# Weight sums, extra products and a second rotation input in the Householder phase of a fused rotation and transformer kernel

## The chip, the core and the metric

The kernel runs on one core of one Trainium2 chip. The metric is the device time of one execution in microseconds (us). Three runs of the kernel before took 2220.52, 2226.43 and 2232.18 us; their median, 2226.43 us, is the time before. Everything is computed in 32-bit floating point.

## The reference

A batch of 8 sequences of 512 tokens with 576 features is first rotated in a subspace and then goes through one transformer block whose shifts, scales and gates come from a conditioning vector. Cut to what matters:

```python
U, _ = jnp.linalg.qr(P)                       # P: 576 x 64
A    = skew-symmetric 64 x 64 from silu(cond) @ W.T + b     # one per sequence
R    = expm(A)
z    = einsum('btn,nd->btd', x, U)
x    = x + einsum('btd,nd->btn', einsum('btd,bde->bte', z, R) - z, U)
ada  = silu(c) @ ada_w + ada_b                # 6 x 576: shifts, scales, gates
x    = x + gate_msa * attention(modulate(layernorm(x)))     # over the 16 heads of one token
x    = x + gate_mlp * (gelu(modulate(layernorm(x)) @ fc1_w + fc1_b) @ fc2_w + fc2_b)
```

The attention is not over tokens: each token has a 16 x 16 matrix of scores between its own heads, which the kernel makes on VectorE. The MLP's inner width is 2304.

## The kernel before

**The prologue.** The factor U comes from a Householder QR of P, written out in 64 steps (`qr_step`, L217 to L285). Each step has two small TensorE products, `rp` (L220, a row spread over all partitions) and `dp` (L228, column sums by a matrix of ones), a chain of small VectorE instructions (L237 to L283, then the next step's products and sums in `column_products`, L209 and L214), and two ScalarE instructions (L244, L245). A step needs the one before it, so the prologue's length is the sum of the steps.

Between two steps a generator, `beside` (L450), is asked for one piece of other work, which lands in TensorE's queue after the step's `dp` and before the next step's `rp`: the 9 column groups of `ada` (`ada_columns`, L306; five products of 384 columns each), the 8 groups of skew entries (`skew_entries`, L337), the rows of the skew matrices by way of DRAM (`skew_rows`, L349), the modulation columns (`modulation`, L317), and the matrix exponential (`expm`, L370): polynomial terms made on GpSimd, and 19 squarings, each of two products of 64 x 64 blocks (`products`, L362) whose results are copied by ScalarE (L444) and get a constant added by GpSimd (L446). The generator's work ends five steps before the QR does. The order of TensorE, VectorE and ScalarE in the prologue is the order in which the code is written; GpSimd and the DMA queue (SP) are ordered by the framework's planner[...].

After the 64 steps a triangular inverse is made in six levels (L513 to L539), then U and its transpose (L549, L556).

**The block.** Work goes unit by unit: (sequence 0, tile 0), (0, 1), (0, tiles 2 and 3), and then two units of two tiles of 128 tokens for each of the other seven sequences. A unit has the projection of its attention output (`Projection`, L756), a norm, and the MLP; beside it run the qkv products of the next unit (`qkv`, L685), the rotation of the next sequence (`rotation`, L622: `project_z` reads x transposed, `rotate` reads x), and, on VectorE, the attention of the next unit (`attention`, L708). The attention output goes to DRAM (L750) and is read back in another layout (L771); both transfers are issued by SP's queue.

The MLP exists in two forms. `mlp_plain` (L870) makes fc2 with 8 products of 288 columns for each of 9 pairs of blocks and two tiles. `mlp` (L907) is a Strassen-like scheme: 4 products of 288 and 4 of 144 columns per pair, and one of 288 at the end, with sums of activation blocks made on GpSimd (L923 to L926) and sums of fc2's weight blocks read from a DRAM buffer, `comb_d` (L933). Sequence 0 uses `mlp_plain`, the other sequences `mlp`. In the unit of sequence 0 that has two tiles, `mlp_plain` also makes the weight sums, four GpSimd instructions for each pair (`combine_weights`, L859), and stores them to `comb_d` (L868).

From the first unit on, the planner orders every engine. One buffer holds the rotation's transposed input `xT` (L635), five hold normed tokens, and one DMA queue (SP's) carries every transfer.

Of the kernel before, what the change touches and what calls it, by code (L numbers as in the profile page):

```python
# [48 lines left out]
def rotate_then_dit_block(  # L49
# [64 lines left out]
    with tc.manual_schedule(engines=engines), tc.tile_pool(name="prep", bufs=1) as prep, tc.tile_pool(name="qrs", bufs=2) as qrs, tc.tile_pool(  # L114
# [4 lines left out]
        name="ps_ex", bufs=2, space=PSUM  # L119
    ) as ps_ex, tc.tile_pool(name="ps_m", bufs=2, space=PSUM) as ps_m:  # L120
        m = prep.tile([128, NK, R], F32, tag="m", name="m")
# [166 lines left out]
        def paced(n, parts):  # L288

            k = 0  # L290
            for part in parts:
                for _ in part:
                    k += 1
                    if k % n == 0:
                        yield
# [10 lines left out]
        def ada_columns(g):  # L306
# [6 lines left out]
            for k in range(2):  # L313
                if g == (4, 8)[k]:
                    nc.sync.dma_start(out=gates_d[k], in_=ada_rows[:, (3 * k + 2) * D : (3 * k + 3) * D])

        def modulation(v):  # L317
            ps = ps_m.tile([128, NK, B], F32, tag="m", name=f"mod_{v}")
            for c, rows in enumerate(KROWS):
                first = v * D + c * 128  # L320
                nc.tensor.matmul(
                    ps[0:rows, c], lhsT=ada_rows[:, first : first + rows], rhs=ident[0:B, 0:B], start=True, stop=True
                )
            for c0, c1, rows in ((0, 4, 128), (4, 5, 64)):
                dst = mod[0:rows, v // 3 * 2 + v % 3, c0:c1, :]
                if v % 3:
                    nc.scalar.activation(dst, ps[0:rows, c0:c1], AF.Identity, bias=ones[0:rows, 0:1])
                else:
                    nc.scalar.copy(dst, ps[0:rows, c0:c1])
# [120 lines left out]
        def beside():  # L450
            yield
            yield
            yield from paced(4, [ada_columns(g) for g in range(6)])
            yield from paced(4, [skew_entries(g) for g in range(8)])
            skew_rows()
            for v in (0, 1, 3):
                modulation(v)
                yield
            yield
            yield from expm()  # L460
            yield from paced(2, [ada_columns(g) for g in range(6, 9)])
            modulation(4)
            yield

        for g in range(4):
# [9 lines left out]
        for j in range(R):  # L475
            t, done = qr_step(j, t, done)
            if j > 1:
                next(side, None)
            if j == 8:
                load_rows(wqkv, qkv_w, 65)  # L480
                nc.sync.dma_start(out=b2, in_=fc2_b.to_broadcast([128, D]))
                for g in (6, 7, 8):
                    load_ada(g)
        for _ in side:
            pass

# [3 lines left out]
        if True:  # L490
# [24 lines left out]
            nc.vector.scalar_tensor_tensor(ls[1], vv, rd, lower[1], ALU.mult, ALU.mult)  # L515
            nc.vector.tensor_tensor(y_, ident[0:R, 0:R], ls[1], ALU.subtract)
            xps = ps_m.tile([R, R], F32, tag="m", name="xps")
            nc.tensor.matmul(xps, lhsT=y_, rhs=ident[0:R, 0:R], start=True, stop=True)
# [9 lines left out]
            for s in LEVELS[1:]:  # L528
                p1 = ps_qr.tile([R, R], F32, tag="dp", name=f"p1_{s}")
                nc.tensor.matmul(p1, lhsT=ls[s], rhs=x_, start=True, stop=True)  # L530
                p1s = qrs.tile([R, R], F32, tag="p1s", name=f"p1s_{s}")
                nc.vector.tensor_copy(p1s, p1)
                p2t = ps_m.tile([R, R], F32, tag="m", name=f"p2t_{s}")
                nc.tensor.matmul(p2t, lhsT=p1s, rhs=y_, start=True, stop=True)
                if s < LEVELS[-1]:
                    p2 = ps_m.tile([R, R], F32, tag="m", name=f"p2_{s}")
                    nc.tensor.matmul(p2, lhsT=y_, rhs=p1s, start=True, stop=True)
                    nc.vector.tensor_tensor(x_, x_, p2, ALU.subtract)
                nc.vector.tensor_tensor(y_, y_, p2t, ALU.subtract)  # L539


            ps = ps_m.tile([R, R], F32, tag="m", name="s_ps")
            nc.tensor.matmul(ps, lhsT=y_, rhs=vt[:, 0:R], start=True, stop=True)
            sneg = prep.tile([R, 2, R], F32, tag="sneg", name="sneg")
            for h in range(2):
# [39 lines left out]

    xns = padded("xn", 5)
    ats = padded("at", 2)
# [34 lines left out]
    def rotation(b):  # L622


        def project_z(half):
            if half == 0:
                zTs[b] = big.tile([128, S], F32, tag="zT", name=f"zT_{b}")
                p = slice(b // 4 * R, b // 4 * R + R)
                for n in range(2):
# [4 lines left out]
                    nc.scalar.copy(g[0:R, n * HALF : (n + 1) * HALF], gps)  # L634
            xT = xin.tile([128, NK, 256], F32, tag="xT", name=f"xT_{b}_{half}")  # L635
            cols = slice(half * 256, half * 256 + 256)
# [71 lines left out]
    def attention(b, ts):  # L708
# [5 lines left out]
        own = [toks.pop((b, i)) for i in ts]  # L714
        sc2 = small.tile([128, 2, H, H], F32, tag="sc", name=f"sc_{hb}", bufs=2)[:, 0:NU]
        for t, tok in enumerate(own):
# [141 lines left out]

    def combine_weights(g, w2):  # L859

        (b11, b12), (b21, b22) = [(w[:, 0:HALF], w[:, HALF:D]) for w in w2]
        tt = wst.tile([128, 3, HALF], F32, tag="w2t", name=f"tt_{g}", bufs=3)
        t1, t2, t4 = (tt[:, k] for k in range(3))
        nc.gpsimd.tensor_tensor(t1, b12, b11, ALU.subtract)
        nc.gpsimd.tensor_tensor(t2, b22, t1, ALU.subtract)
        nc.gpsimd.tensor_tensor(t3[:, g], b22, b12, ALU.subtract)
        nc.gpsimd.tensor_tensor(t4, t2, b21, ALU.subtract)
        nc.sync.dma_start(out=comb_d[g], in_=tt)  # L868

    def mlp_plain(pr, gate, aside):  # L870
        hb, NU = pr.hb, len(pr.ts)
        acc, gts = {}, {}
        for g in range(NP + 1):
# [8 lines left out]
            for k in range(2):  # L882
# [6 lines left out]
                for t in range(NU):  # L889
                    for n in range(2):  # L890
# [8 lines left out]
                        )  # L899
            if NU == 2:  # L900
                combine_weights(g, w2)
        for t in range(NU):
# [4 lines left out]
    def mlp(pr, gate, aside):  # L907
# [8 lines left out]
        for g in range(NP + 1):  # L916
# [18 lines left out]
            stop = g == NP - 1  # L935
            whole = [(gt[:, 0, 0], wq[:, 0]), (gt[:, 1, 0], wq[:, 1]), (ss[:, 2], wq[:, 2]), (gt[:, 1, 1], wt[:, 2])]
            for k in (0, 1, 3):
                nc.tensor.matmul(p[k], lhsT=whole[k][0], rhs=whole[k][1], start=g == 0, stop=stop)  # L938

            nc.tensor.matmul(p[2], lhsT=whole[2][0], rhs=whole[2][1], start=g == 0, stop=stop)  # L940
            for i, (lhs, rhs) in ((5, (ss[:, 0], wt[:, 0])), (6, (ss[:, 1], wt[:, 1]))):
                for n, bank in enumerate(halves_of[i]):
# [50 lines left out]
    first = rotation(0)  # L993
    now(first[:3])
    feature_major(0, 0)
    now(qkv(0, 0))
    now(first[3:])
    now(qkv(0, 1))
# [4 lines left out]
    for k, (b, ts) in enumerate(units):  # L1003
# [10 lines left out]
        else:  # L1014
            nb, nts = units[k + 1]
            q = qkv(nb, nts[0]) + qkv(nb, nts[1])
        if len(ts) == 1:
            pr.turn(0)
            now(q[:1])
            pr.product(0, 0)  # L1020
            pr.product(0, 1)
            pr.norm(0, gb2)
            now(q[1:3])
            pr.turn_normed((0, 1))
            now(q[3:])
        else:
# [16 lines left out]
        if (k == 1 or k > 2 and ts[0] == 0) and b + 1 < B:  # L1043
# [3 lines left out]
            aside |= {7: lambda: feature_major(b + 1, 0), 8: lambda: feature_major(b + 1, 1)}  # L1047
        (mlp if b else mlp_plain)(pr, gate_m, aside)
        if k + 1 < len(units):
# [54 lines left out]
```

## Time and profile before

| | |
|---|---|
| median of three runs | 2226.43 us (2220.52 to 2232.18) |
| the profiled execution, its own time | 2228.81 us |
| its span, first to last instruction | 2227.0 us |
| mean granted TensorE clock over the span | 0.952 |
| TensorE (PE) busy | 2104.2 us, 94% |
| VectorE (DVE) busy | 1789.4 us, 80% |
| GpSimd (POOL) busy | 679.6 us, 31% |
| ScalarE (ACT) busy | 386.7 us, 17% |
| DMA | 347.58 MB, mean 156 GB/s |

The span falls into three parts: the prologue up to about 247 us, the start of the block up to about 647 us, and a long even part up to the end. A busy share over the whole span says little about the first two. PE is TensorE's products and PEld its loading of the stationary operand; "PEclk" is the clock that the chip granted to TensorE. A product in 32-bit floating point shows as two instruction records. Where a group of records carries a count such as x8, the time is that of the whole group. In the chain of waits each line is the start, the length and what the chain ran through.

### The profile page before, as it was taken

How to read it: one execution, taken by the hardware profiler on the slowest of the kernel's cores; microseconds unless marked ns; L12 is line 12 of the kernel's file. 1: busy time of each engine (PE TensorE's matmuls, PEld its weight loads, DVE VectorE, ACT ScalarE, POOL GpSimd, SP SyncE). 2: the span in 40 equal slices, each digit the busy share in tenths (PEclk: the TensorE clock that was granted, in tenths of full speed). 3: DMA queues.
4: the chain of work that ended last, by engine and by line, in shares of the span. 5: the costliest groups of instructions: out<-in, count | busy, mean ns of one | idle time of the engine just before them, and what ended most of it. 6: DMA issues, size and time to landing. Idle time of an engine off the chain costs nothing.

```text
span 2227.0 us, 26157 instructions
## 1 busy us (share of the span) xinstructions
PE 2104.2 (94%) x9571; PEld 1570.8 (71%) x9571; DVE 1789.4 (80%) x2443; ACT 386.7 (17%) x817; POOL 679.6 (31%) x846
## 2 busy tenths in 40 slices
PE   7788879899799999999999999999999999999998
PEld 3485437666568686868687777777786868686877
DVE  8997399899678797969796979697988889697930
ACT  2232111122021111111111112121211122111110
POOL 2151000113434242424242433324332334242422
PEclk9755789999999999999999999999999999999999
DMA  9101116743647373845565465637373737364654
GB/s 304 30 2 62 50 54 206 249 124 111 186 156 233 107 214 108 251 128 170 155 201 165 153 178 168 205 116 208 128 231 98 215 114 225 111 202 122 200 178 125
DMA packets 211698, 347.58 MB, mean 156 GB/s; under 512 B 82382, under 2 KB 100123, under 8 KB 211572
## 3 DMA queue, kind: packets, MB, share of 16 engines
q1 hardware_dynamic: 211572, 345.92, 51.3%
q8 instruction: 77, 1.26, 0.2%
q14 instruction: 49, 0.40, 0.1%
HBM read 313.46 MB, written 32.39 MB: 155 GB/s over the span
## 4 chain that ended last, share of the span: by engine, by line
PE 65%; DVE 14%; issue 11%; DMA 6%; POOL 3%; ACT 1%; SPq 0%; POOLq 0%; DVEq 0%; ACTq 0%
PE fc L838 26%; PE fc L938 8%; PE qkvp L696 7%; PE fc L943 5%; DVE sc L727 3%; PE fc L940 3%; PE p L953 3%; DMA w<-in_fc_w 3%; PE fc L893 2%; PE ada L310 2%; DMA out<-x 1%; DVE qk L721 1%; PE zps L640 1%; DVE pv L743 1%; DVE att L749 1%
## 5 line engine op out<-in xcount | busy, mean ns | idle before, releaser
L838 PE MATMUL fc<-h2T,w 128*128 128x256 f32 (+3 forms) x3060 | 656.4, 368 | 2.0 <-ACT h2T L814 1.9
L838 PEld LDWEIGHTS fc<-h2T,w 128*128 128x128 f32 (+1 forms) x3060 | 549.4, 191 | 76.8 <-ACT h2T L814 7.0
L696 PE MATMUL qkvp<-wqkv,hT 128*128 128x432 f32 (+1 forms) x1280 | 480.9, 529 | 1.3 <-DVE pt L795 0.9
L721 DVE TENSOR_TENSOR qk<-qkv 128x2304 f32<-128x2304 f32 x128 | 327.3, 2557 | 122.9 <-ACT qkv L703 120.4
L696 PEld LDWEIGHTS qkvp<-wqkv,hT 128*128 128x128 f32 (+1 forms) x1280 | 240.6, 191 | 204.5 <-issue 196.4
L743 DVE TENSOR_TENSOR pv<-sc,qkv 128x2304 f32<-128x2304 f32 x128 | 330.9, 2585 | 3.3
L749 DVE TENSOR_REDUCE att<-pv 128x144 f32<-128x2304 f32 x128 | 326.5, 2551 | 3.3
L727 DVE TENSOR_REDUCE sc<-qk 128x64 f32<-128x2304 f32 x128 | 326.3, 2549 | 2.8
L923 POOL TENSOR_TENSOR ss<-gt 128x128 f32<-128x128 f32 x126 | 135.1, 1072 | 539.4 <-ACT gt L846 539.4
L846 ACT ACTIVATE gt<-fc 128x512 f32<-128x512 f32 (+1 forms) x153 | 87.5, 572 | 725.2 <-PE fc L838 725.0
L703 ACT COPY qkv<-qkvp 128x432 f32<-128x432 f32 x128 | 66.3, 518 | 559.0 <-PE qkvp L696 552.6
L943 PEld LDWEIGHTS fc<-wt,ss 128*128 128x128 f32 x1008 | 140.5, 190 | 13.2
L943 PE MATMUL fc<-wt,ss 128*128 128x144 f32 x1008 | 144.1, 286 | 0.0
L938 PE MATMUL fc<-wq,gt 128*128 128x288 f32 x504 | 142.8, 405 | 0.0
L610 POOL TENSOR_TENSOR rstd_m<-rstd_m,mhalf 128x1 f32<-128x1 f32 x32 | 17.6, 551 | 362.0 <-DVE rstd_m L609 338.3
L969 DVE TENSOR_TENSOR u<-u,fc 128x288 f32<-128x288 f32 x14 | 6.4, 454 | 135.3 <-ACT u L968 135.3
L793 PE MATMUL pj<-w2q_p,aT 128*128 128x288 f32 x384 | 108.5, 419 | 4.0 <-DMA w2q_p<-in_proj_w 2.3
L938 PEld LDWEIGHTS fc<-wq,gt 128*128 128x128 f32 x504 | 94.1, 189 | 19.9
L854 POOL TENSOR_TENSOR x<-x,mt 128x288 f32<-128x288 f32 x64 | 50.8, 796 | 169.5 <-DVE mt L853 169.5
L893 PE MATMUL fc<-w,gt 128*128 128x288 f32 x288 | 82.6, 431 | 20.4 <-DMA w<-in_fc_w 19.8
L925 POOL TENSOR_TENSOR ss<-gt,ss 128x128 f32<-128x128 f32 x126 | 97.7, 776 | 9.9
L793 PEld LDWEIGHTS pj<-w2q_p,aT 128*128 128x128 f32 x384 | 71.7, 194 | 31.5 <-issue 6.2
(223 smaller groups left out, 2381.1 us busy)
## 6 DMA issues: line engine op xcount, KB each, us to landing
w<-in_fc_w SPq DMA_DIRECT2D x306, 320.0 KB, 3.4
wq<-in_fc_q SPq DMA_DIRECT2D x126, 432.0 KB, 3.7
wt<-comb_d SPq DMA_DIRECT2D x126, 432.0 KB, 4.2
w<-in_fc_w SPq DMA_DIRECT2D x54, 288.0 KB, 4.1
w2q_p<-in_proj_w SPq DMA_DIRECT2D x34, 432.0 KB, 3.7
xT<-in_x_t SPq DMA_DIRECT2D x16, 640.0 KB, 10.1
w2t_p<-in_proj_w SPq DMA_DIRECT2D x34, 288.0 KB, 3.3
xt<-in_x SPq DMA_DIRECT2D x32, 288.0 KB, 2.8
```

The costliest lines, as they stand in the source:

```text
L696: nc.tensor.matmul(ps, lhsT=hT[0:k, c, i * 128 : (i + 1) * 128], rhs=wqkv[0:k, c, n * N : (n + 1) * N], start=c == 0, stop=c == NK - 1,)
L721: nc.vector.tensor_tensor(pr, q[:, c * HC : (c + 1) * HC].unsqueeze(2).to_broadcast([128, HC, H, DH]), k.unsqueeze(1).to_broadcast([128, H ...
L727: nc.vector.tensor_reduce(sc2[:, t, c * HC : (c + 1) * HC, :], pr, AX.X, ALU.add)
L743: nc.vector.tensor_tensor(pr, sc2[:, t, c * HC : (c + 1) * HC, :].unsqueeze(2).to_broadcast([128, HC, DH, H]), v.unsqueeze(1).to_broadcast ...
L749: nc.vector.tensor_reduce(att[:, c * HC : (c + 1) * HC, :], pr, AX.X, ALU.add)
L793: nc.tensor.matmul(ps, lhsT=aT[0:k, c, :], rhs=w, start=c == 0, stop=c == NK - 1)
L838: nc.tensor.matmul(ps[:, k], lhsT=w1[0:n, c, :], rhs=h2T[0:n, c, 0 : NU * 128], start=c == 0, stop=c == NK - 1,)
L893: nc.tensor.matmul(acc[t, n][:, 0:HALF], lhsT=gts[g][:, k, t], rhs=w2[k][:, n * HALF : (n + 1) * HALF], start=g + k == 0, stop=g == NP - 1 ...
L923: nc.gpsimd.tensor_tensor(ss[:, 0], gt[:, 0, 1], gt[:, 1, 1], ALU.add)
L925: nc.gpsimd.tensor_tensor(ss[:, 2], gt[:, 1, 0], ss[:, 1], ALU.subtract)
L938: nc.tensor.matmul(p[k], lhsT=whole[k][0], rhs=whole[k][1], start=g == 0, stop=stop)
L943: nc.tensor.matmul(bank[:, side], lhsT=lhs, rhs=rhs[:, n * QUARTER : (n + 1) * QUARTER], start=False, stop=stop, skip_group_check=True,)
```

## The change

Five things are changed.

1. Products of the identity with itself, whose results nobody reads, are put between the steps (`stream(n)`, n times 128 columns): 49 of them, in the first six requests to `beside`, beside the modulations, beside the later squarings, in the last eleven steps, and between the products of the triangular inverse.
2. The groups 6 to 8 of `ada` no longer follow the exponential, two products to a step; one of their 15 products goes beside each of the first 15 steps of the exponential. Their weights are loaded in steps 20, 24 and 28, not in step 8.
3. The sums of fc2's weight blocks are made during steps 13 to 31, in the buffers of the `ada` weights: for each of 9 pairs two loads of rows of fc2, four GpSimd instructions, and two stores to `comb_d`. `combine_weights` goes away, and the unit (0, tiles 2 and 3) uses `mlp` and no longer `mlp_plain`.
4. `xT` gets two buffers, and the first four pieces of the first rotation come before the first transposes. Normed tokens get four buffers and no longer five, scores one and no longer two.
5. In the units of one tile the next tile's first three groups of qkv come before the projection.

```diff
@@ the prologue's functions
+        def weight_sums(g):
+            w = sums[g] = adap.tile([128, NK, AC], F32, tag="aw", name=f"w2_{g}")
+            w = w.rearrange("p c n -> p (c n)")[:, 0 : 4 * HALF].rearrange("p (k c) -> p k c", c=HALF)
+            for k in range(2):
+                rows = fc2_w[(g + k * NP) * 128 : (g + k * NP + 1) * 128]
+                nc.sync.dma_start(out=w[:, 2 * k : 2 * k + 2].rearrange("p k c -> p (k c)"), in_=rows)
+            b11, b12, b21, b22 = (w[:, k] for k in range(4))
+            nc.gpsimd.tensor_tensor(t3[:, g], b22, b12, ALU.subtract)
+            nc.gpsimd.tensor_tensor(b11, b12, b11, ALU.subtract)
+            nc.gpsimd.tensor_tensor(b22, b22, b11, ALU.subtract)
+            nc.gpsimd.tensor_tensor(b21, b22, b21, ALU.subtract)
+
+        def store_sums(g):
+            w = sums.pop(g).rearrange("p c n -> p (c n)")
+            nc.sync.dma_start(out=comb_d[g][:, 0], in_=w[:, 0:HALF])
+            nc.sync.dma_start(out=comb_d[g][:, 1:3].rearrange("p k c -> p (k c)"), in_=w[:, 2 * HALF : 4 * HALF])
+
+        def stream(n):
+            ps = ps_s.tile([128, 512], F32, tag="s", name=f"s_{next(count)}")
+            nc.tensor.matmul(
+                ps[:, 0 : n * 128],
+                lhsT=ident,
+                rhs=ident.unsqueeze(1).to_broadcast([128, n, 128]),
+                start=True,
+                stop=True,
+            )
...
         def beside():
-            yield
-            yield
+            stream(4)
+            for _ in range(5):
+                stream(4)
+                stream(4)
+                yield
             yield from paced(4, [ada_columns(g) for g in range(6)])
             yield from paced(4, [skew_entries(g) for g in range(8)])
             skew_rows()
             for v in (0, 1, 3):
                 modulation(v)
+                stream(4)
                 yield
+            stream(4)
+            stream(2)
             yield
-            yield from expm()
-            yield from paced(2, [ada_columns(g) for g in range(6, 9)])
+            rest = paced(1, [ada_columns(g) for g in range(6, 9)])
+            for _ in expm():
+                if next(rest, 0) == 0:
+                    stream(2)
+                yield
+            for _ in rest:
+                yield
             modulation(4)
             yield
+            while True:
+                stream(4)
+                yield
...
             t, done = qr_step(j, t, done)
-            if j > 1:
-                next(side, None)
+            next(side)
+            if j % 2 and 12 < j < 33:
+                g = (j - 13) // 2
+                if g < NP:
+                    weight_sums(g)
+                if g > 0:
+                    store_sums(g - 1)
             if j == 8:
                 load_rows(wqkv, qkv_w, 65)
                 nc.sync.dma_start(out=b2, in_=fc2_b.to_broadcast([128, D]))
-                for g in (6, 7, 8):
-                    load_ada(g)
-        for _ in side:
-            pass
+            if j in (20, 24, 28):
+                load_ada(j // 4 + 1)
@@ the triangular inverse: stream(2) before xps, stream(1) after p1, stream(2) after p2 and after s_ps
...
-    xns = padded("xn", 5)
+    xns = padded("xn", 4)
...
-            xT = xin.tile([128, NK, 256], F32, tag="xT", name=f"xT_{b}_{half}")
+            xT = xin.tile([128, NK, 256], F32, tag="xT", name=f"xT_{b}_{half}", bufs=2)
...
-        sc2 = small.tile([128, 2, H, H], F32, tag="sc", name=f"sc_{hb}", bufs=2)[:, 0:NU]
+        sc2 = small.tile([128, 2, H, H], F32, tag="sc", name=f"sc_{hb}", bufs=1)[:, 0:NU]
...
     first = rotation(0)
-    now(first[:3])
+    now(first[:4])
     feature_major(0, 0)
     now(qkv(0, 0))
-    now(first[3:])
+    now(first[4:])
...
         if len(ts) == 1:
+            now(q[:3])
             pr.turn(0)
-            now(q[:1])
             pr.product(0, 0)
             pr.product(0, 1)
             pr.norm(0, gb2)
-            now(q[1:3])
+            now(q[3:])
             pr.turn_normed((0, 1))
-            now(q[3:])
...
-        (mlp if b else mlp_plain)(pr, gate_m, aside)
+        (mlp if len(ts) == 2 else mlp_plain)(pr, gate_m, aside)
```

`mlp` reads the three stored sums at their new places in `comb_d`, and `combine_weights` is deleted.

## The prediction

> **What bounds the kernel now.** I read the page's slices first, then one answer that cuts the span into five stretches (length, busy time and instruction count of each engine, granted clock as a share of full, share of the DMA engines, GB/s).
>
> ```profile
> span 2227.0 us, 26157 instructions
> ...
> PE   7788879899799999999999999999999999999998
> ...
> PEclk9755789999999999999999999999999999999999
> ```
>
> ```profile
> 0.00:219.40 219.40, 174.55 (x1172) 116.16 (x1172) 187.48 (x1079) 55.62 (x200) 57.73 (x123) 0.69 0.31 101
> 219.40:271.00 51.60, 40.49 (x130) 23.63 (x131) 13.55 (x62) 7.70 (x20) 4.07 (x18) 0.66 0.15 48
> 271.00:593.60 322.60, 285.81 (x1241) 203.08 (x1240) 298.70 (x209) 55.33 (x106) 59.38 (x47) 0.96 0.48 147
> 593.60:647.20 53.60, 42.79 (x149) 27.25 (x148) 19.87 (x28) 6.90 (x15) 16.32 (x17) 0.94 0.61 182
> 647.20:2227.00 1579.80, 1560.59 (x6884) 1200.67 (x6884) 1269.78 (x1069) 261.17 (x477) 542.13 (x642) 1.00 0.56 168
> ```
>
> The Householder steps take 219.4 us at a clock of 0.69; the inverse, U and the first rotation 51.6 us at 0.66; then VectorE's attention of sequence 0 and of the first half of sequence 1 sets the pace (298.7 of 322.6 us busy); a gap of 53.6 us follows in which PE waits and VectorE has little; from 647.2 PE is 99% busy. What happens before 593.6 therefore shifts all that follows one for one. The last stretch has 19 us of idle PE and no edit aims at it.
>
> **The clock** is 1.0 or 0.5 and changes only on a grid of 3.413 us. Some such stretches:
>
> ```profile
> 80.31:83.73 3.42, 2.33 (x18) 2.03 (x18) 3.22 (x19) 0.98 (x6) 0.00 (x0) 1.00 0.18 24
> 189.54:192.95 3.41, 3.41 (x9) 1.30 (x8) 2.04 (x14) 0.73 (x3) 0.00 (x0) 0.50 0.67 257
> 390.93:394.34 3.41, 1.50 (x7) 0.70 (x5) 2.16 (x5) 2.04 (x3) 0.74 (x1) 1.00 0.85 307
> 394.34:397.75 3.41, 2.96 (x6) 2.19 (x7) 0.39 (x1) 0.42 (x1) 1.04 (x2) 0.50 0.62 168
> 565.01:568.42 3.41, 1.54 (x6) 1.25 (x7) 3.38 (x2) 0.00 (x0) 1.46 (x2) 1.00 1.15 261
> ```
>
> The clock fell after the first and third stretch, rose after the fourth, stayed in the second and fifth. I weighed each by streamed columns, against 4096 that full speed would stream in 3.413 us (a product over 64 rows counted half): falls at shares of 0.06 to 0.36 (0.36 in the third), none at 0.37 (the fifth) or more; at half clock no rise up to 0.71 of the half rate, a rise at 0.79 (the fourth). One limit near 0.36 of full speed, some 1,500 columns, fits all. **A rule against a row:** the Trainium skill (TensorE: Matmul & The Clock Gate, "Why this matters for your kernels") asks for no idle gap of PE over about 3 us. Row one has PE busy in 2.33 of 3.42 us, so no such gap, and the clock fell. By the rule the streams hold full clock everywhere (time under the rivals); by the limit only where a step streams enough. I take the limit. A product of 32-bit data streams twice: 128 columns take 0.21 us at full clock, 0.43 at half, so a stream of 4 takes 0.85 or 1.71.
>
> **The change, part by part** (minus is a gain).
>
> *Steps 0 to 9.* Three streams of 512 in step 0 last 5.1 us at half clock, under it a step of about 3.8: +1.0. The clock is up before the first `ada` step, which took 5.0 us at half clock and would take 3.5; about 0.2 us in each of four steps before. Sum −1.1 (bounds −4, +3).
>
> *Weight sums in steps 13 to 31.* 36 GpSimd instructions, 36 transfers. VectorE's small instructions with two inputs in SBUF wait for a running GpSimd one:
>
> ```profile
> 90.43 0.15 DVE L257 TENSOR_TENSOR m<-m,dg 128x1 f32<-128x1 f32 x1
> ...
> 151.63 0.72 POOL L446 TENSOR_TENSOR ex_f<-ex_f,ex_i 128x256 f32<-128x256 f32 x1
> ...
> 151.74 0.63 DVE L257 TENSOR_TENSOR m<-m,dg 128x1 f32<-128x1 f32 x1
> ...
> 499.96 2.48 POOL L865 TENSOR_TENSOR tt<-w,tt 128x288 f32<-128x288 f32 x1 [31.84 <-DMA w<-in_fc_w]
> ```
>
> The skill says so too (SBUF — State Buffer, "Who interferes with whom"): the two contend through an exclusive lock, the loser blocked wholly. If each of the 36 sums (median 0.79 us, groups L864 to L867) blocked for its whole length, that is +28. Measured, VectorE's excess from 93 to 181 us is 13.3 us over 55 GpSimd instructions, 0.24 each: 36 x 0.24 = 9, less what falls in waits for PE. I take +8, bounds +3 and +13. The loads lie on an SP queue with little in it (101 GB/s). New waits: each pair's stores wait for its sums; behind them on SP are the next pair's loads, the `ada` groups 6 to 8 and the store of the skew rows. A pair takes load 4.1 + sums 3.2, overlapped over two steps of 3.3 us, so the skew rows would be issued near 86 us (81.4 now), back near 90, with their first reader near 100. I cost it at nothing; past that cover it is a rival.
>
> *Modulations and the exponential's start.* A modulation step with its stream has 1024 columns and the small products in 3.3 us, 0.31: the clock falls there as now. The polynomial steps (30.2 us for seven) wait on GpSimd; they now get an `ada` product of 1.28 us at half clock and the last sums: +4 (0 to +8).
>
> *Squarings* (2.9 to 3.2 us a step, PE full: 1.9 products + 0.4 `rp` + 0.6 `dp`). With an `ada` product a step at half clock is 4.2 us at 0.76 of the half rate, between 0.71 and 0.79, so I take it that the clock rises after two such steps, which then take about 2.8: net 0 (up to +8.4 if it doesn't rise). Steps 42 to 50 with streams of 256 at full clock take 2.6 against 2.9: −3. Steps 51 and 52, no longer squarings: −2.
>
> *Last eleven steps.* Now 35.5 us, since seven carry two `ada` products each (3.6 to 4.4) and the bare ones take 2.30 at half clock. After: a step with no stream (52) lets the clock fall, and 512 columns in a step at half clock give 2.70 us (1.71 + `rp` + `dp`), 29.7: −6 (−12.4 if the clock holds: 2.1 each; 0 if a stream hides less).
>
> *Inverse and first rotation.* The clock is half from 194 to 247 us. After the streams beside the inverse's first products it should be full in u (2.6), ut (2.1), gps (2.1), zps (4.6), each nearly halved: −6 (−1 to −8). PE is idle from 250.06 to 252.15 and from 252.6 to 254.2, waiting for the second `xT`, and the clock falls at 254.4; with two buffers the second `zps` fills the gap: −3.2 (0 to −5).
>
> *The unit (0, tiles 2 and 3) and after.* The chain of waits there:
>
> ```profile
> 594.12 6.84 DMA att<-att
> 600.98 0.53 SPq L771
> 601.60 3.81 DMA w<-in_fc_w
> 605.54 2.40 PE fc L893 x8
> 607.94 4.52 DMA w<-in_fc_w
> 612.50 3.90 PE fc L893 x8
> 616.40 0.55 PE atr L782 x5
> ```
>
> Four loads of fc2 blocks stand in SP's queue behind the attention's read-back of sequence 1, which waits for VectorE, so this unit's MLP can't end before 616.4. After the change no `comb_d` store waits on GpSimd in that unit, and all of its loads but the last group's stand before the read-back of (1, tiles 2 and 3). Then PE is free when that lands at 602: the chain from `atr` moves by 616.4 − 602 = 14.4 us at most, and part of the 11.2 us of qkv products inside it can be done in the idle time: +3 more. Cap: PE's idle time in the unit (2.7 + 2.3 + 3.6 + 4.2 + 4.6 = 17.4) and the 9 products of 288 that `mlp` saves (2 x 0.24 each, 4.3), 21.7. I take −17, bounds −8 and −22. GpSimd makes 36 activation sums of 0.455 there in place of 36 of 0.79 us.
>
> *Rest.* Fewer normed tokens, one buffer of scores, a second `xT`: every reader is in a stretch where PE is 99% busy and VectorE 80%; a ring that stalls would be seen as PE idle. 0 (−3 to +3).
>
> Sum: −1.1 + 8 + 4 − 3 − 2 − 6 − 6 − 3.2 − 17 = −26.3. The profiled execution took 2228.8 (1.8 beside its span) and lies 2.4 above the median: 2202.5 in its terms, **2200** in the median's. A measurement here tells about 0.5%, 11 us, from no change.
>
> **Rivals.**
> *A, clock held everywhere* (the rule): −12.4 for −6 in the last steps, 0 for +4, some −8 more in steps 26 to 40: about 2181. For it: the streams are in nearly all steps; against: the first row shown. Chance 0.12.
> *B, clock lost through the squarings*: +8.4 there, +7 where 42 to 51 stay at half, +3 on the last steps: 2219. For it: 0.76 is not measured. 0.15.
> *C, unit gain absent*: PE's idle time moves from the end of the unit to the wait for attention, since VectorE still ends near 593.6 less the prologue's 9: 2217. For it: VectorE is the pace until then; against: 14 us between landing and `atr`. 0.07.
> *D, slower*: the sums' chain on SP and GpSimd delays the skew rows. Seven pairs stand before their store, one pair is asked for in two steps (6.6 us), and the rows have 10 us of cover. At p us a pair they are 7 x (p − 6.6) late; the exponential waits from p = 8, and the whole forecast gain of 26 us is gone at p = 11.7. With a load of 4.1 and four sums of 2.5, nothing overlapped, p is 14.1: 52 us late, 42 on the path, about 2242. For it: the sum at 499.96 took 2.48 us; against: VectorE ran instructions of 2.5 us there, in the steps they are under 1 us, and the median is 0.79. 0.06.
> *Forecast*: 0.60, own range 2190 to 2212.
>
> **Chances and range.** Faster by over 0.5% (under 2215.3): forecast 0.58, A 0.12, parts of B and C 0.08: 0.78. Same: 0.15. Slower: 0.07. The range reaches over A and B: 2178 to 2223.
>
> **What would show it.** Right: clock near 1.0 in the first 80 us, falling at the modulations and at step 52; VectorE's L257 and L238 longer in steps 13 to 31; attention starting near 261.5 and still gapless; the next unit's first L838 near 620 in place of 647.15 (−9 − 17); PE 99% busy after. Wrong: skew entries arriving after 95 us, squarings at half clock, a PE gap of over 10 us before `atr`, or idle PE in the even part.

## The result and the profile after

The changed kernel is not faster. Over 20 runs it took 2230.97 us (2227.51 to 2236.05) beside 2223.47 us (2216.86 to 2235.01) of the kernel before: a ratio of 1.0028, with an interval of 1.0014 to 1.0042. Forecast were 2200 us. The profiled executions stand closer, with spans of 2228.5 and 2227.0 us: the runs of before fall into two groups, ten from 2216.9 to 2221.2 and ten from 2225.8 to 2235.0, and its profile is one of the upper group.

The page of the changed kernel:

```profile
span 2228.5 us, 26469 instructions
...
PE   8878997899989999999999999999999999999998
...
PEclk9768798999999999999999999999999999999999
```

Five stretches of it (columns as in the prediction: length, busy time of PE, PEld, DVE, ACT, POOL, granted clock, DMA share, GB/s):

```profile
0.00:239.90 239.90, 195.86 (x1247) 111.77 (x1247) 206.08 (x1080) 55.46 (x200) 86.06 (x159) 0.79 0.41 134
239.90:293.70 53.80, 49.15 (x162) 28.75 (x162) 13.32 (x61) 7.97 (x21) 3.96 (x16) 0.75 0.17 58
293.70:599.50 305.80, 277.12 (x1232) 199.75 (x1231) 281.69 (x203) 55.06 (x106) 46.18 (x50) 0.96 0.55 160
599.50:648.30 48.80, 42.78 (x168) 29.04 (x166) 37.60 (x43) 7.37 (x16) 10.19 (x13) 0.93 0.49 129
648.30:2228.50 1580.20, 1561.49 (x6884) 1201.47 (x6884) 1269.55 (x1069) 261.44 (x477) 540.68 (x642) 1.00 0.58 168
```

The cuts are the start of the last Householder step, the start of VectorE's attention, the end of its 24th group, and the first product of fc1 in the first unit of sequence 1. All but the third are the same events as before. Before, the 24th group ended at 577.94; the cut at 593.6 lay behind three more groups of scores, those of the next unit. So the third and the fourth line can't be compared one by one with those of before, only their sum can.

The Householder steps end 20.5 us later than before, at a clock that is higher (0.79 for 0.69; these views count the time ahead of the first clock record as full, 10.4 us here and 25.7 us before, and with it at half, as the first products ran, it is 0.76 for 0.63). VectorE's attention begins at 293.74, 22.9 us later than before. From there to the first product of fc1 in the first unit of sequence 1 (648.28) it is 354.5 us, where it was 376.3 us (270.82 to 647.15): a gain of 21.8. The even part is as it was (1580.2 for 1579.8). 22.9 − 21.8 + 0.4 = 1.5 us, the difference of the spans. The gain in the block came, a little larger than forecast; the prologue, which was to gain 9 us, ate it.

The start of VectorE's first instruction on `rp` marks each Householder step, and the length of a step is the time from the start of the one before it to its own. From these starts, the prologue piece by piece, one execution each:

| piece | before, us | after, us | difference | forecast |
|---|---|---|---|---|
| start to step 10 | 44.5 | 43.2 | −1.4 | −1.1 |
| steps 11 to 23 (most sums) | 42.3 | 55.8 | +13.6 | +8 |
| steps 24 to 26 (modulations) | 9.7 | 13.2 | +3.5 | 0 |
| steps 27 to 34 (exponential's start) | 33.4 | 37.8 | +4.5 | +4 |
| steps 35 to 50 (squarings) | 47.7 | 57.9 | +10.2 | −3 |
| steps 51 and 52 | 6.4 | 5.5 | −0.9 | −2 |
| last eleven steps | 35.5 | 26.5 | −9.0 | −6 |
| last step to start of u | 16.1 | 20.6 | +4.4 | −6 with the next row |
| u to end of the first `zps` | 11.5 | 10.4 | −1.0 | |
| to the attention | 23.8 | 22.8 | −1.0 | −3 |

Three rows are far off: the sums in size, the squarings and the inverse (ahead of u) in sign. Where the time lies is seen in single steps. Step 13 of the changed kernel, VectorE and GpSimd alone (start, length, engine, line, what; x2 is the time of two instructions together):

```profile
52.30 0.81 DVE L275 TENSOR_TENSOR up<-m,w 128x130 f32<-128x130 f32 x1
53.04 1.81 DVE L285 SCALAR_TENSOR_TENSOR m<-up,r,m 128x125 f32<-128x125 f32 x2
53.04 0.79 POOL L331 TENSOR_TENSOR w<-w 128x288 f32<-128x288 f32 x1
53.91 0.79 POOL L332 TENSOR_TENSOR w<-w 128x288 f32<-128x288 f32 x1
54.66 0.84 POOL L330 TENSOR_TENSOR w<-w 128x288 f32<-128x288 f32 x1
54.77 1.67 DVE L211 TENSOR_TENSOR pr<-m 128x125 f32<-128x125 f32 x2
...
56.37 0.64 DVE L216 TENSOR_REDUCE t<-pr 128x25 f32<-128x125 f32 x2
```

GpSimd's sums run back to back under it. The instructions with two inputs in SBUF (`m`, `pr`, `up`) take three times what they take without, and more (0.60, 0.48 and 0.27, shown below in the first run); the reduction `t`, with one input, takes the same. The step took 6.87 us in place of 3.33.

A squaring step of the changed kernel at full clock (step 38):

```profile
161.69 0.68 PE L403 MATMUL pe<-ex_e,ex_f 64*64 64x64 f32 x16
...
162.76 0.81 PE L312 MATMUL ada<-aw,sc 128*8 128x384 f32 x2
162.81 0.99 DVE L285 SCALAR_TENSOR_TENSOR m<-up,r,m 128x65 f32<-128x65 f32 x2
...
162.99 0.72 POOL L482 TENSOR_TENSOR ex_e<-ex_e,ex_i 128x256 f32<-128x256 f32 x1 [2.33 <-PE pf L403]
163.67 0.72 POOL L482 TENSOR_TENSOR ex_f<-ex_f,ex_i 128x256 f32<-128x256 f32 x1
163.72 0.89 DVE L211 TENSOR_TENSOR pr<-m 128x65 f32<-128x65 f32 x2
163.85 0.40 PE L222 MATMUL rp<-m,ident 128*128 128x26 f32 x2 [0.28 <-DVE m L285]
```

And one of the kernel before, at half clock:

```profile
160.36 0.72 POOL L446 TENSOR_TENSOR ex_e<-ex_e,ex_i 128x256 f32<-128x256 f32 x1
...
160.44 0.65 DVE L257 TENSOR_TENSOR m<-m,dg 128x1 f32<-128x1 f32 x1
160.46 1.12 PE L367 MATMUL pe<-ex_e,ex_f 64*64 64x64 f32 x16
...
161.37 1.06 PE L367 MATMUL pf<-ex_f,ex_e 64*64 64x64 f32 x16
161.66 0.45 DVE L283 SCALAR_TENSOR_TENSOR m<-up,r,m 128x45 f32<-128x45 f32 x2
162.02 0.33 DVE L209 TENSOR_TENSOR pr<-m 128x45 f32<-128x45 f32 x2
162.36 0.61 PE L220 MATMUL rp<-m,ident 128*128 128x19 f32 x2
```

Before, the products fill PE's time until `rp`, and GpSimd's additions fall under work that is not last: 2.9 us a step. After, the products are done by 163.6, `rp` waits for VectorE's `m`, and the additions fall on just the two pairs of wide instructions: 3.7 us a step. Full clock came, as forecast, but the step was no longer PE's.

The inverse, in the chain of waits, one level before (from `p` to the next `p`, 1.78 us):

```profile
227.85 0.49 PE p L530 x2
...
229.63 0.49 PE p L530 x2
```

and after, 2.89 us, with no wait between the products at all:

```profile
250.07 1.15 PE s L343 x2
251.22 0.40 PE p L584 x2
251.62 0.72 PE s L343 x2
252.34 0.40 PE p2t L589 x2
...
252.96 1.15 PE s L343 x2
```

`s` is a stream. At half clock it outlasts the wait that it was to fill, and the clock didn't rise: it fell at 245.9 and rose at 269.8.

### The profile page after: what moved, and what is told of

It reads as the page before. It is cut to its first block, busy times and chain, and to the rows that moved or that the text cites. A ratio compares the mean times of both kernels' runs of the same rounds, so it can differ in the third digit from the quotient of the medians.

```text
span 2228.5 us, 26469 instructions
## 1 busy us (share of the span) xinstructions
PE 2126.4 (95%) x9687; PEld 1570.8 (70%) x9687; DVE 1808.2 (81%) x2453; ACT 387.3 (17%) x818; POOL 687.1 (31%) x880
## 4 chain that ended last, share of the span: by engine, by line
PE 58%; DVE 22%; issue 11%; DMA 5%; POOL 2%; ACT 1%; SPq 0%; POOLq 0%; DVEq 0%; ACTq 0%
PE fc L895 24%; PE fc L982 7%; PE qkvp L753 5%; PE fc L987 5%; DVE sc L784 4%; DVE pv L800 3%; DVE att L806 3%; DVE qk L778 3%; PE fc L984 2%; PE p L997 2%; PE s L343 2%; PE zps L697 2%; DMA out<-x 1%; PE fc L939 1%; PE rot L705 1%
## 5 line engine op out<-in xcount | busy, mean ns | idle before, releaser
L967 POOL TENSOR_TENSOR ss<-gt 128x128 f32<-128x128 f32 x135 | 143.7, 1065 | 577.2 <-ACT gt L903 577.2
L987 PEld LDWEIGHTS fc<-wt,ss 128*128 128x128 f32 x1080 | 150.5, 190 | 14.2
L987 PE MATMUL fc<-wt,ss 128*128 128x144 f32 x1080 | 154.4, 286 | 0.0
L982 PE MATMUL fc<-wq,gt 128*128 128x288 f32 x540 | 153.0, 405 | 0.0
L982 PEld LDWEIGHTS fc<-wq,gt 128*128 128x128 f32 x540 | 100.8, 189 | 21.3
L969 POOL TENSOR_TENSOR ss<-gt,ss 128x128 f32<-128x128 f32 x135 | 104.2, 772 | 10.6
L970 POOL TENSOR_TENSOR s<-gt 128x128 f32<-128x128 f32 x135 | 92.6, 686 | 0.0
```

Of the source, the lines that this page charges most:

```text
L967: nc.gpsimd.tensor_tensor(ss[:, 0], gt[:, 0, 1], gt[:, 1, 1], ALU.add)
L969: nc.gpsimd.tensor_tensor(ss[:, 2], gt[:, 1, 0], ss[:, 1], ALU.subtract)
L970: nc.gpsimd.tensor_tensor(s3s[g], gt[:, 0, 0], gt[:, 0, 1], ALU.subtract)
L987: nc.tensor.matmul(bank[:, side], lhsT=lhs, rhs=rhs[:, n * QUARTER : (n + 1) * QUARTER], start=False, stop=stop, skip_group_check=True,)
```

## The experiments

The theory after the result: what was gained in the block was lost in three places of the prologue, to GpSimd's sums that block VectorE, to squarings that at full clock are VectorE's and not PE's, and to streams on the path.

**1. No sums.** The four GpSimd instructions of `weight_sums` are left out; `t3` is zero and what is stored are plain rows of fc2.

```diff
-            b11, b12, b21, b22 = (w[:, k] for k in range(4))
-            nc.gpsimd.tensor_tensor(t3[:, g], b22, b12, ALU.subtract)
...
+        nc.gpsimd.memset(t3, 0.0)
```

> The changed kernel without the 36 GpSimd instructions of the weight sums; the loads and the stores to DRAM stay, so wrong sums are stored, and t3 is zero. Theory (the GpSimd sums block VectorE's instructions with two inputs in SBUF): steps 12 to 25 take again what they took before the change (3.1 to 3.6 us each in place of 3.7 to 6.9), the last Householder step starts 13 to 18 us earlier than 239.9, the time falls from 2231 to about 2215. Rival (the transfers beside the steps, or the streams, stretch them): under 3 us of change, steps 13 to 20 stay above 3.7 us.

Measured: 2220.12 us, ratio 0.9976 (0.9959 to 0.9994) to the kernel before. Step 20 begins at 76.8 in place of 89.5, the last step at 226.0 in place of 239.9. Step 13 of this run, 3.60 us:

```profile
51.79 0.27 DVE L275 TENSOR_TENSOR up<-m,w 128x130 f32<-128x130 f32 x1
51.98 0.60 DVE L285 SCALAR_TENSOR_TENSOR m<-up,r,m 128x125 f32<-128x125 f32 x2
52.51 0.48 DVE L211 TENSOR_TENSOR pr<-m 128x125 f32<-128x125 f32 x2
52.91 0.64 DVE L216 TENSOR_REDUCE t<-pr 128x25 f32<-128x125 f32 x2
```

All 36 transfers are still there, so it was not they. The price of a sum is 13.9 us over 36, 0.39 each. Part of it may come by a detour that isn't measured apart: in steps 13 to 18 of the changed kernel PE waits for the late VectorE, and the clock falls at 58.1 and at 78.6; without the sums it stays at full through step 23. The time fell 5 us less than expected: of the 13.9 us 12.4 reach the start of the attention (281.32) and 10.8 the span.

**2. No streams.**

```diff
         def stream(n):
+            return
```

> The changed kernel with no stream at all. Theory (the streams lie on the path wherever PE sets the step, and full clock buys little since VectorE's chain then sets it): steps 1 to 5 +1 us, steps 24 to 26 -4, the squaring steps 35 to 40 (an ada product at half clock) +3, steps 41 to 51 back to 2.9 us each, -8, the inverse -5: about 2216. Rival (the streams hold the clock and pay for themselves): slower than the changed kernel by 5 us or more, 2236 or above.

Measured: 2223.24 us, ratio 0.9978 (0.9964 to 0.9993): under the changed kernel by 7.7 us in the medians, 8.0 in the spans and 11 by the two ratios, where 15 were expected. Steps 24 to 26 take 10.2 us in place of 13.2, steps 41 to 51 take 32.6 in place of 38.0, the last step to the attention 49.8 in place of 53.9; the first steps give back 1.8 and steps 35 to 40 give back 1.3. So the streams as a whole cost more than they bring. The rival falls.

**3. No streams in the inverse.**

```diff
-            stream(2)
             xps = ps_m.tile([R, R], F32, tag="m", name="xps")
...
-                stream(1)
                 p1s = qrs.tile([R, R], F32, tag="p1s", name=f"p1s_{s}")
```

> The changed kernel without the four kinds of stream in and around the triangular inverse. Theory: each of four levels goes back from 2.90 to 1.77 us and the stream after s_ps frees 0.7 us, so the attention of the first tile starts 4.5 to 6 us earlier than 293.7; u, ut and gps take the same time, since the clock was at half there anyway. Time about 2226. Rival (as predicted: the streams hold the clock): u, ut, gps and zps grow, and the time is the same or up to 3 us longer.

Measured: a ratio of 1.0008 (0.9990 to 1.0026), 2229.89 us. This interval overlaps the changed kernel's, so the time alone doesn't show a gain; the trace does. The attention starts at 289.67, 4.1 us earlier than with them. The chain of waits has a level of 1.77 us again (247.34 to 249.11), and the products after the inverse:

```profile
247.34 0.48 PE p L583 x2
...
249.11 0.48 PE p L583 x2
...
255.03 2.58 PE u L602 x10
257.61 2.21 PE ut L609 x4
259.82 2.11 PE gps L684 x4
261.93 4.58 PE zps L693 x10
```

The first three take what they take with the streams (2.50, 2.21, 2.11); only `zps` loses 1.0 us of clock (4.58 for 3.61). Of 4.1 us at the attention 2.0 are left in the span. From the start of the attention to the first product `p` (L997 of the changed kernel, the last of the MLP) in the first unit of sequence 1, called the block's stretch below, it takes 434.4 us in place of 431.1, as in runs 1, 2 and 4 (433.6 to 434.5). Why stays open: an earlier start alone is not it, since runs 5 and 9 to 11 start earlier too and take 428.2 to 431.3.

**4. The exponential as before.**

```diff
-            rest = paced(1, [ada_columns(g) for g in range(6, 9)])
-            for _ in expm():
-                if next(rest, 0) == 0:
-                    stream(2)
-                yield
+            yield from expm()
+            yield from paced(2, [ada_columns(g) for g in range(6, 9)])
```

> The changed kernel with the exponential as before: no ada product and no stream beside it, the ada groups 6 to 8 after it, two products a step. Theory (a squaring step at full clock is VectorE's chain of about 2.6 us and two GpSimd adds that block it, about 3.7 us together; at half clock with an ada product or a stream it is PE's, 3.7 us too; without either it is PE's 2.9 us): steps 35 to 48 take 2.9 us each, -10 us; steps 26 to 34 -5; the last steps take 3.6 us again where they have two products, +9. Sum -6: 2225. Rival (clock alone sets the squarings): they get longer at half clock, and the time rises by 5 us or more.

Measured: 2221.03 us, ratio 0.9965 (0.9942 to 0.9988). Steps 35 to 50 take 47.5 us in place of 57.9, the theory's 10 us, at half clock throughout; steps 27 to 34 take 35.3 in place of 37.8. The expected price at the end, +9, did not come: the last eleven steps take 26.7 us (26.5 with the changed order), with two `ada` products in most of them, because the clock rose at 201.7, as they began. In the profile of before these steps stayed at half clock and took 3.6 us each. The stretch ahead of the rise streams 0.74 of the half rate, those of before, from 179 to 219 us, 0.73 at most.

**5. No additions.** ScalarE copies the squared product a second time where GpSimd added 2I, so the exponential is wrong.

```diff
-                        nc.gpsimd.tensor_tensor(plus, src, i2, ALU.add)
+                        nc.scalar.copy(plus, ps)
```

> The changed kernel with the addition of 2I after each squaring left out: ScalarE copies the product a second time in its place, so the exponential is wrong; the order and the number of products stay. Theory (at full clock two GpSimd adds per step block VectorE's wide instructions on its chain): the squaring steps at full clock take 2.6 to 3.0 us in place of 3.7, those at half clock with an ada product or a stream stay at 3.7 or more, since PE sets them. Rival (PE or ScalarE sets the steps at full clock too): they stay at 3.6 to 3.8 us.

Measured once, without an interval: 2210.71 us, span 2209.0. The clock is full from 150.0 to 197.8, and the squarings take 2.78 us falling to 2.42. In step 38:

```profile
159.92 0.48 DVE L285 SCALAR_TENSOR_TENSOR m<-up,r,m 128x65 f32<-128x65 f32 x2
160.32 0.35 DVE L211 TENSOR_TENSOR pr<-m 128x65 f32<-128x65 f32 x2
```

`m` takes 0.48 in place of 0.99 and `pr` 0.35 in place of 0.89: 1.05 us for two additions of 0.72, and the step is 1.0 us shorter (2.68 for 3.72). PE has the same products here and ScalarE two copies more, so neither of them set the steps. Nor did the products wait for the additions: the second one ended at 164.39 in the step shown above, the next products begin at 165.4. The expected half did not hold: no step of these stayed at 3.7, since with shorter steps the same products stream a larger share, and the clock did not fall.

**6 and 7. The sums in another place.** The prologue of the kernel before; `combine_weights` runs in the unit (0, tile 1), and (0, tiles 2 and 3) uses `mlp`. The second of the two has all other edits to the block too.

```diff
-            if NU == 2:
+            if pr.ts == (1,):
                 combine_weights(g, w2)
...
-        (mlp if b else mlp_plain)(pr, gate_m, aside)
+        (mlp if len(ts) == 2 else mlp_plain)(pr, gate_m, aside)
```

> The kernel before with one part of the change alone, and the sums in another place: combine_weights is called in the unit (0, tile 1) and no longer in (0, tiles 2 and 3), which uses mlp. Prologue as before. Theory (the gain of some 18 us in that unit comes from its MLP having no sums and stores of its own, while the prologue took it back): the attention starts near 270.8 as before, the next unit's first product of fc1 18 us earlier than 647, so a time 18 us under the kernel before, a ratio of 0.992. Rival (most of the gain comes from xT's second buffer and the qkv order, or the sums only move the wait into unit (0, tile 1)): under 6 us of gain, a ratio of 0.997 or above.

> The run above with the rest of the change's edits to the block: two buffers of xT and first[:4], four normed tokens, one buffer of scores, the qkv groups before the projection. Theory: these are worth under 4 us beside the run above, either way. Rival (they carry the gain): 10 us or more below the run above.

Measured: 2212.84 us, ratio 0.9947 (0.9925 to 0.9970), and 2204.42 us, ratio 0.9922 (0.9900 to 0.9945). Both are under both kernels. The first gains 12 of the 18 us that were expected. The block's stretch takes 441.5 and 444.0 us: 452.9 before, 431.1 in the changed kernel. VectorE's first 24 groups of attention take 315.6 and 318.6 us in place of the changed kernel's 305.7, with nearly the same work (283.2, 284.4 and 281.7 us of VectorE); the difference is idle time. In the first run 13.2 us of it lie between 437 and 476 us, while the sums run on GpSimd (400.8 to 476.8), where the same stretch of the changed kernel has 4.7; the longest wait, 7.0 us, is for a product of fc2 of that unit. Much of the wait moved there. The intervals of the two runs overlap, and the traced execution of the second is the slowest of its fourteen (2219.47 us). Among the executions of both with a mean clock of 0.956 or more the medians are 2205.2 (8) and 2204.0 us (10), so the other edits to the block are worth little; the attention starts 2.4 us earlier with them (269.26 for 271.64).

**8. Both repairs.** Run 7 with the early streams, one stream of 512 in the first step that has two `ada` products after the exponential, and the streams of the bare steps.

```diff
             yield from expm()
+            stream(4)
             yield from paced(2, [ada_columns(g) for g in range(6, 9)])
```

> A version from what the runs show: the run with the sums in unit (0, tile 1) and all of the change's edits to the block; in the steps the exponential as before, and of the streams only the early ones, one of 512 columns in the first step that has two ada products after the exponential (to raise the clock), and those of the bare steps. Theory: early streams -1.5 us, the seven steps with two ada products near 2.4 us each in place of 3.6 at full clock, -8, the attention starts near 260; with the unit's gain 2193 to 2203, ratio 0.986 to 0.991. Rival (the clock falls again in these steps, as where the stream of 512 is over too soon): attention near 268, ratio 0.992 or more.

Measured: 2210.21 us, ratio 0.9931 (0.9913 to 0.9949), not distinguishable from run 7. The last step starts at 213.9 in place of 220.2 and the attention at 263.5, but the clock rose two steps late (the step with the stream took 5.44 us, the next 3.62, then 2.2 to 2.4), and the median isn't below run 7's. Neither theory nor rival is met in full: the attention came where half way between them lies. Why the median doesn't follow is open; what the faster executions of run 7 do in the prologue was not traced.

**9 and 10. Sums after the inverse.** `weight_sums` and `store_sums` for all pairs are written after the product `s_ps`, in run 8's prologue and in that of before.

```diff
             nc.tensor.matmul(ps, lhsT=y_, rhs=vt[:, 0:R], start=True, stop=True)
+            for g in range(NP):
+                weight_sums(g)
+                store_sums(g)
```

> The version of run e8_combo with the weight sums neither in unit (0, tile 1) nor in the steps but after the triangular inverse, as weight_sums and store_sums for all nine pairs, where VectorE has 13.6 us of work in 51.6. Theory (the sums cost what they block of a VectorE that sets the pace): the steps as in that run (last one near 214), the attention at most 4 us later after the last step than 49.6 us, and the stretch from there to the first p7 of a Strassen-like MLP back from 441.6 to 431 to 435 us; time 2196 to 2204, ratio 0.987 to 0.991. Rival (the 36 sums stand on GpSimd before the norms' rstd and hold the block's first buffers): the attention starts 15 us or more later, ratio 0.995 or above.

> The prologue as before, without any stream, with the weight sums after the triangular inverse, and all of the change's edits to the block. Theory: the attention starts near 270 to 274, the stretch to the first p7 takes 431 to 435 us; 18 us under the kernel before, ratio 0.990 to 0.993; run e9_late_sums is below it by what its steps save, 4 to 7 us. Rival: as for that run, ratio 0.997 or above.

Measured: ratios 0.9941 (0.9915 to 0.9967) and 0.9930 (0.9902 to 0.9958), from five and four runs. The eight executions of the kernel before beside them have a median of 2229.44 us, where it is 2225.82 beside runs 5 to 8, so these two ratios are some 0.0015 low beside the others. They did not do what they were for. GpSimd's order is the planner's, the sums wait for nothing but their loads, and in run 10 they ran from 60 to 171 us, amid the steps. The last step starts at 230.6 in run 9 where run 8 has 213.9 (+16.7, 0.46 us for each of 36 sums), and at 232.7 in run 10 where run 7 has 220.2; these 12.6 us hold a gain of 6.1 us in the last eleven steps, where the clock rose at 214.4, and without it a sum costs 0.52. In steps 13 to 23 the price is 0.45 and 0.48 (12 sums each), in the squaring steps, at half clock, 0.65 and 0.62 (12 each). The block's stretch then takes 428.2 and 431.3 us, as in the changed kernel.

**11. Sums held.** Run 8 with a copy of the last column of `m` into each tile ahead of its load, so that loads and sums wait for the last step.

```diff
+            for k in range(4):
+                nc.gpsimd.tensor_copy(w[0:R, k, 0:1], after[:, 0:1])
```

> Run e8_combo with the weight sums held until the Householder steps are done: for each pair four copies of 64 elements from the last column of m go ahead of the loads, on GpSimd, into the tiles that are loaded. The sums then lie beside the inverse, U and the first qkv products, where VectorE has 13.6 us of work in 51.6; nine pairs at 3.3 us and the first load end some 35 us after the last step, and the first norm's rstd stands behind them on GpSimd. Theory: no step is lengthened (last one near 214), the attention starts up to 6 us later than in that run, 264 to 270, the stretch from there to the first p7 is 431 to 435 us in place of 441.6: the first p7 at 697 to 704 in place of 705.1, ratio 0.987 to 0.992. Rival (the waits on GpSimd move the norms by more than the sums cost in unit (0, tile 1)): attention after 273, ratio 0.994 or more.

Measured: 2217.0 us, ratio 0.9965 (0.9950 to 0.9981); the rival's case. No step is longer (the last starts at 212.3) and the block's stretch takes 430.8 us, but the attention starts at 279.9, 16.4 us later than in run 8. Its chain of waits:

```profile
254.13 0.32 SPq L339
...
254.55 0.38 SPq L642
...
254.98 6.40 DMA gate<-gates_d
...
261.44 1.40 POOL gb L1039
262.84 0.53 POOL rstd_a L655
263.39 0.59 DVE xn L656
```

The load of a gate stands in SP's queue behind the last store of the sums (L339), the product `gb` that reads it stands on GpSimd ahead of the second tile's `rstd`, and that norm stands before the first qkv products. The sums lengthen no step here, but they hold two queues.

## Why the prediction was wrong

- *What bounds the kernel, and the shift one for one*: right. 22.9 us later at the attention and 21.8 us less behind it make up the spans.
- *The unit (0, tiles 2 and 3)*: right in the cause, SP's queue behind the sums; −17 forecast and −21.8 measured. Runs 9 to 11 show it with other prologues, and runs 6 and 7 show that it needs the sums out of the units. One step was misread: the end of the attention, whose landing near 602 was to set the pace, was put at 593.6. The 24th group ended at 577.94; its store to DRAM stood 16 us in SP's queue, behind stores of the sums (L868) that waited for GpSimd. In the kernel before:

```profile
575.39 2.55 DVE L749 TENSOR_REDUCE att<-pv 128x144 f32<-128x2304 f32 x1
...
593.22 0.33 SPq L868 DMA_DIRECT2D comb_d<-tt  x1
593.61 0.42 SPq L835 DMA_DIRECT2D w<-in_fc_w  x1
594.12 0.58 SPq L750 DMA_DIRECT2D att<-att  x1
```

These stores waited 15.9 us in two waits between 577 and 602 us. After the change the last group ends at 599.5 and its store goes at 600.00. Counted from the attention's start, the read-back is issued 15.6 us earlier than before and `atr` starts 27.4 us earlier, beyond the 14.4 that were set as the most; then PE waits 6.0 us for `pt` (L852), as scores of the next unit stand ahead of it on VectorE. That the sum came close to its cap of 22 is in part luck.

- *Weight sums, +8*: the mechanism was named, the size was off: 13.9 us (run 1), over the upper bound of 13. The step that failed is "0.24 each", an average over the additions between 93 and 181 us (the trace has 59 GpSimd instructions of 256 columns there, the prediction says 55). Of the 13 us that VectorE loses there, about 6.4 lie on L257 and 5.0 on L238, two small instructions just behind `rp`: the additions wait for the squared products and so fall there, as in the step of before shown above. The sums wait only for their loads, and run over the wide instructions too (step 13). That PE set the pace there is not the reason: in the squaring steps of runs 9 and 10, also at half clock, a sum cost 0.62 to 0.65 (how much of that came by sums holding up the additions on GpSimd was not measured apart). Of the two numbers that were weighed, the lock for the whole length (0.79, +28) and the row (0.24, +9), 0.39 lies between, nearer to the row.
- *Squarings, 0 and then −3*: the step that failed is "which then take about 2.8" and "steps 42 to 50 at full clock take 2.6". The clock rose about as said, at 153.7 (it was at half once more from 174.2 to 187.8); the steps took 3.7 us. VectorE's chain of 2.7 us had been seen only while PE was last, so the additions' blocks were costed at nothing. Run 5 removes them and finds 2.4 to 2.8. The prediction applied the blocking to the instructions that the change added and not to those already there, whose cover the change took away. At half clock, with a product or a stream beside them, the steps take 3.7 us too (run 4 takes that away: 2.9).
- *Modulations, nothing*: the step "the clock falls there as now" was right, and with it a stream of 512 lies on PE's path at 2.0 us, which the sum left out though it had the price of 1.71: +3.5.
- *Inverse to `zps`, −6*: wrong. The products of the inverse are over 64 rows and the levels wait for VectorE; with the streams the stretches of 3.413 us from 245.9 to 259.5 came to 0.46 to 0.56 of the half rate (the same counting as in the prediction), far under the 0.74 of the lowest rise, so the clock stayed at half and the streams only added 4.4 us (run 3: 4.1). The limit was there; it wasn't applied.
- *First rotation, −3.2*: −1.0. The reading was wrong: from 250.06 to 252.15 and from 252.6 to 254.2 PE waited for the norm's `xn` and not for the second `xT`. The gap was PE's and not the path's: from the end of the first `zps` to the transpose of the second norm's output it is 7.2 us before and after, through the norm's `rstd` on GpSimd and `xn` on VectorE.
- *Early steps, exponential's start, last steps, rest*: −1.4, +4.5, −9.0 and +0.4, for −1.1, +4, −6 and 0. In the last steps the clock fell at 215.2 as forecast, and the streams raised it again from 225.4 to 232.2.
- *The rivals*: none was right. A fails with the clock falling at 58.1, 78.6, 99.1, 174.2 and 215.2. B names the place, the squarings, but not the cause: they were slow at full clock. D, the slower one, asked whether the sums come late; the skew rows were back by 103.5, later than the 95 that was to be a warning, but their first reader ran at 112.5, so nothing waited for them. What the sums cost was VectorE's time. The rule on idle gaps against the limit in streamed columns: the limit holds (last section).

## What to carry to other kernels

When a faster clock or a shorter product takes one engine off the path, cost the next engine's chain with everything that blocks it, the instructions that were there before included: their blocks were free only while another engine was last. A price per instruction has to come from instructions that fall on the same place of the chain: 0.24 us for additions that mostly fell on two small instructions became 0.39 to 0.52 for sums that fell anywhere. Filler products to hold a clock belong where PE waits longer than they last at half clock. And GpSimd work that is moved should go where VectorE has no wide two-input instructions on its path, with a dependency that keeps it there, since its program position doesn't, and where nothing on the path stands behind it on GpSimd or in a DMA queue (run 11).

## What was not expected

- A late VectorE lowers PE's clock: with the sums, the stretch from 54.7 to 58.1 us streamed 0.15 of full speed and the clock fell in step 14; without them it was full from step 1 through step 23.
- The clock's limit is narrow, and the same number of columns in both states. Counted over all stretches of 3.413 us up to 2100 us of the thirteen traces, with each product's columns weighed by its rows out of 128, the clock fell (126 times) at shares of full speed up to 0.39 and was kept from 0.375 on; it rose (139 times) at 0.74 of the half rate and above (0.37 of full), while stretches of up to 0.76 (0.38 of full) didn't raise it. The small overlaps may be the error of the count.
- Steps with two `ada` products lie at this limit: they stayed at half clock for eight steps of 3.6 us in the profile of before, and rose to full in run 4, where they take 2.2 to 2.4 us. That this also makes the two groups of executions of the kernel before is likely and was not shown: of the 52 beside runs 1 to 4, 25 have a mean clock of 0.957 and a median of 2220.9 us, 27 have 0.950 and 2232.3 us. The clocks differ by about 28 us at half rate, which is what eight steps of 3.6 us are.
